# An attention and quantised-FFN layer on one core: loads spread, first queries stored first, roots moved to GpSimd, and two moves in the order of work

## The chip, the cores and the metric

The kernel runs on one core of a Trainium2 chip. The core has five engines with a queue of instructions each: TensorE (PE; its weight loads are shown as PEld), VectorE (DVE), ScalarE (ACT), GpSimd (POOL) and SyncE (SP, which here only issues transfers). Transfers are carried by 16 DMA engines; SP and POOL both issue them. An engine takes its instructions in order, and one that waits holds up all behind it. The metric is the device time of one execution in microseconds; the kernel before takes 1176.38 us (median of 3 runs, 1175.61 to 1177.49).

## The reference

`x` is (2, 1024, 512) in float32: two batches of 1024 tokens. Two layers follow each other, each on the layer norm of its input and added to it:

```python
q, k, v = proj(w_q), proj(w_k), proj(w_v)          # 32 heads of 16
attn = softmax(q @ k.T / sqrt(16))
x = x + (attn @ v) @ w_o.T

xq = int4_quant(layernorm(x))                      # rounded, clipped to -8..7
gate, up = bitlinear(xq, w_gate), bitlinear(xq, w_up)   # 512 -> 1376, weights -1, 0, 1
inter = int8_quant(up * square(relu(gate)))
x = x + bitlinear(inter, w_down)                   # 1376 -> 512
```

`int4_quant` divides by the mean absolute value of a row (beta), `int8_quant` by its largest absolute value (gamma). `bitlinear` divides a weight matrix by its mean absolute value (`w_mean`), rounds to -1, 0 or 1, and multiplies the product by `w_mean` and a scale. `w_mean` is needed of the three matrices before their first use.

## The kernel before

**Steps and slots.** The attention is cut into 32 steps: a batch, a half of its 512 queries (h), a group of 8 heads (g) and one half of that group (s), 4 heads at a time on PE. A step has 8 slots. In a slot T of the loop at the end of the kernel, PE computes scores for the maxima of one step (`max_mm`, L635, tiles `psm`), the scores for the exponentials of an older step, ten slots behind (`exp_mm`, L670, `pse`), and the products with the values of a still older one (L703, `pso`). DVE reduces `psm` to maxima (L645), ACT computes the exponentials `e` (L680). Scores stand in three pairs of PSUM banks, which are used in turn.

**Where the operands come from.** Projected queries and keys are split in a high and a low part (`hi`, `lo`) and stored to DRAM (`qD`, `kD`, L507 and L510), the values to `vD`; they come back in the layouts that the steps need: `kst` and `qst` for the maxima (L574, L580), `kw` (keys, two halves of four slots, L599) and `qm` (queries, L606) for the exponentials, `v` (L611), which POOL spreads into `vk` (L616). A step's row maxima become extra rows of `qm`: DVE combines them (`max_parts`, L650 to L653), PE transposes them (`max_rows`, L658, `psn`), ACT copies the row (L661) and POOL repeats it (L663).

**The start.** `norm_inputs` normalises the first batch's two halves (`fast`): means and variances on DVE, the inverse root by `inverse_root`, centring, PE transpositions. PE runs 40 warm-up matmuls (L1342) meanwhile. `project_qk` with `first` then projects the first keys and queries, and copies `hi` and `lo` straight into `kst` and `qst` of steps 0 and 1, in pieces of 16 rows (L500), by SP and POOL; after that it stores them to `qD` and `kD` (L507, L510). `upto` runs a generator until it yields a given word, and `now` to its end; their sequence sets the order of SP's and POOL's queues there.

**Fill.** All other work is a set of generators in `Fillers`. `fill.run(budget)` is called twice in a slot, once for short work and once with `share` (ns of PE time), and advances tasks that are ready, by their due slots. `("gap", n)` makes a task sleep for n such calls, so n / 2 slots. The background list holds the sums of the absolute weights (`weight_sums`, 35 blocks of up to 0.25 MB, loaded by POOL, L803, and summed by ACT, L817), then their quantising (`weight_quant`, POOL L859 and DVE L861, blocks loaded by POOL again). `norm_inputs` of the second batch is a task too: eight loads of 0.25 MB on SP (L365). `output_proj` (`psy`, L900, for two tiles of 128 tokens), `ffn_input`, `ffn_product` (gate `pg` and up `pu`, L989) and `ffn_output` (`py`, L1059) make the second layer for 12 of the 16 tiles of tokens. `fill.pace` gives the PE time per slot that meets all due slots; `share` is at least SHARE (960) and at most MORE (1800).

**The end.** The last four tiles are made in `the_end`, whose list (`Line`) is ordered by a planner: each generator names its next instruction's engine and modelled time, and the planner emits the one that can start first.

**The inverse root** (L336 to L353) is a bit trick and three Newton steps, 12 DVE operations on a few columns.

Of the kernel before, what the change touches and what calls it, by code (L numbers as in the profile page):

```python
# [10 lines left out]
F32 = mybir.dt.float32  # L11
# [222 lines left out]
def kernel(  # L234
# [66 lines left out]
    for i in range(4):  # L301
        nc.vector.memset(second[32 * i : 32 * i + 16, :], 0)
    negmagic = const.tile([P, 1], F32, name="negmagic")
# [33 lines left out]
    def inverse_root(dst, var, k, name):  # L337

        a = sp.tile([P, k], F32, tag="ra", name=f"ra_{name}")
        t = sp.tile([P, k], F32, tag="rt", name=f"rt_{name}")  # L340
        y = sp.tile([P, k], F32, tag="ry", name=f"ry_{name}")
        nc.vector.tensor_scalar(a, var, EPS, None, ALU.add)
        nc.vector.tensor_scalar(
            t.bitcast(I32), a.bitcast(I32), 1, None, ALU.logical_shift_right
        )
        nc.vector.tensor_scalar(
            y.bitcast(I32), t.bitcast(I32), -1, RSQRT_SEED, ALU.mult, ALU.add
        )
        for i in range(3):
            yield ("gap", 1, "light")  # L350
            nc.vector.tensor_tensor(t, y, y, ALU.mult)
            nc.vector.scalar_tensor_tensor(t, t, -0.5, a, ALU.mult, ALU.mult)
            nc.vector.scalar_tensor_tensor(dst if i == 2 else y, t, 1.5, y, ALU.add, ALU.mult)  # L353
# [3 lines left out]
    def norm_inputs(b, half, fast, need=()):  # L357
# [8 lines left out]
        yield ("gap", 4 if fast else 14)  # L366
# [10 lines left out]
        yield from inverse_root(r[:, c], mv[:, c, 1], n, f"1_{k}")  # L377
# [85 lines left out]
    def project_qk(b, g, which, h, have, fast=False, first=False):  # L463
# [25 lines left out]
        yield ("gap", 3)  # L489
        if first:  # L490

            for s in range(2 - which):
                for l, part in enumerate((hi, lo)):
                    for a in range(2 - which):
                        for r in range(4):
                            src = part[32 * r + 16 * s : 32 * r + 16 * s + 16, :].bitcast(F32)
                            at = 32 * r + 16 * (l if which else a)
                            dst = kst[0][:, h * QB : (h + 1) * QB] if which else qst[s][l]
                            queue = (nc.sync, nc.gpsimd)[l if which else a]
                            queue.dma_start(dst[at : at + 16, :].bitcast(F32), src)  # L500
                yield ("copied",)
        queue = nc.gpsimd if fast and not first else nc.sync
        for l, part in enumerate((hi, lo)):
# [7 lines left out]
            yield ("gap", 1)  # L511

# [293 lines left out]
    def weight_sums():  # L806
# [5 lines left out]
        for k in range(len(todo) + 4):  # L812
# [12 lines left out]
            yield ("gap", 2)  # L825
# [50 lines left out]
    def output_proj(b, h, tiles):  # L876
# [48 lines left out]
        nc.vector.tensor_scalar(neg, mv[:, :, 0], -1.0, None, ALU.mult)  # L925
        yield from inverse_root(r, mv[:, :, 1], w, f"2_{k}")
# [13 lines left out]
        nc.vector.tensor_scalar(cg, beta, wscale[0], None, ALU.mult)  # L940
        nc.vector.tensor_tensor(cg, cg, cg, ALU.mult)
        nc.vector.scalar_tensor_tensor(c3, beta, wscale[1], cg, ALU.mult, ALU.mult)
# [79 lines left out]

    def ffn_output(b, h, i, last):
# [72 lines left out]
    def the_end(n):  # L1096
# [208 lines left out]
        for k in range(2):  # L1305
            line.add(values(k))
            line.add(scales(k))
# [266 lines left out]
```

## Time and profile before

| | us |
|---|---|
| median of 3 runs | 1176.38 |
| profiled execution | 1175.35 |
| its span, first to last instruction | 1173.5 |
| PE busy | 1122.4 |
| DVE busy | 850.0 |
| ACT busy | 699.5 |
| POOL busy | 370.4 |

Engines overlap, so their busy times don't add up. A slice row of the page has 40 digits, each the busy tenths of 1/40 of the span. A line of waits reads: who waited, for whom, microseconds in total, times, the longest. A line of the chain of waits reads: start, length, and the instruction or transfer that set the time there. A line of the timeline reads: start, length, engine, line of the kernel, operation, tile written and tiles read, count, and in brackets the idle time before it and what ended it.

### The profile page before, as it was taken

What the parts mean: (1) busy time and instruction counts of PE and PEld (TensorE: products, weight loads), DVE (VectorE), ACT (ScalarE), POOL (GpSimd) and SP (SyncE); (2) the same over time, 40 slices, a digit from 0 to 9 for tenths busy, and PEclk for the clock granted to TensorE, in tenths of its full rate; (3) what the DMA queues carried; (4) which work ended last, traced back from release to release, by engine and by line L of the source; (5) the groups of instructions that cost most, each with busy time, mean ns of one, the idle gap of its engine ahead of it and who ended that gap; (6) DMA issues with size and microseconds to landing.
All of it is one profiled execution on the core that took longest, in us unless ns stands there. A gap on an engine that the chain in (4) does not pass through costs nothing.

```text
span 1173.5 us, 18117 instructions
## 1 busy us (share of the span) xinstructions
PE 1122.4 (96%) x6890; PEld 512.7 (44%) x6890; DVE 850.0 (72%) x1291; ACT 699.5 (60%) x894; POOL 370.4 (32%) x433
## 2 busy tenths in 40 slices
PE   8869999699999999999999999999999999999988
PEld 6524545245444545454454333333433434344344
DVE  5836566575877667776666889888888788996257
ACT  2026677476765656566555666666666565676646
POOL 4212234142446554751222123232113122242111
PEclk9889999799999999999999999999999999999999
DMA  5465568656554754655365453667775565543210
GB/s 154 132 154 150 181 182 242 142 147 195 165 141 147 191 157 155 168 167 128 102 174 142 104 116 88 124 132 122 129 114 119 117 127 120 118 96 72 75 27 37
DMA packets 107398, 157.12 MB, mean 134 GB/s; under 512 B 33720, under 2 KB 46488, under 8 KB 107312
## 3 DMA queue, kind: packets, MB, share of 16 engines
q1 hardware_dynamic: 95872, 129.39, 45.8%
q0 software_dynamic: 11440, 26.58, 8.4%
q8 instruction: 54, 0.88, 0.3%
q14 instruction: 32, 0.26, 0.1%
HBM read 114.41 MB, written 34.05 MB: 127 GB/s over the span
## 4 chain that ended last, share of the span: by engine, by line
PE 80%; DVE 10%; DMA 5%; ACT 3%; issue 1%; SPq 1%; POOL 0%; ACTq 0%; POOLq 0%; DVEq 0%
PE pse L670 21%; PE pso L703 18%; PE psm L635 13%; DVE pm L645 7%; PE psk L471 5%; PE psq L471 4%; PE psv L525 4%; PE psy L900 3%; PE py L1059 2%; DMA kw<-kD 2%; PE pu L989 2%; PE pg L989 2%; ACT e L680 1%; PE end L1215 1%; DMA kst<-kD 1%
## 5 line engine op out<-in xcount | busy, mean ns | idle before, releaser
L645 DVE TENSOR_REDUCE pm<-psm 128x2 f32<-128x1024 f32 x512 | 602.2, 1218 | 244.7 <-PE psm L635 243.8
L680 ACT ACTIVATE e<-pse 128x1024 f32<-128x1024 f32 x512 | 524.2, 1026 | 356.7 <-PE pse L670 350.2
L670 PE MATMUL pse<-qm,kw 72*128 72x512 f32 x1024 | 409.6, 483 | 24.5 <-DMA kw<-kD 19.2
L670 PEld LDWEIGHTS pse<-qm,kw 72*128 72x128 f32 x1024 | 169.0, 190 | 307.9 <-ACT e L680 196.9
L703 PE MATMUL pso<-e,vk 128*32 128x512 f32 x2048 | 274.4, 606 | 1.4 <-ACT e L680 1.4
L635 PE MATMUL psm<-kst,qst 32*128 32x512 f32 x2048 | 206.3, 449 | 9.6 <-DVE pm L645 5.1
L635 PEld LDWEIGHTS psm<-kst,qst 32*128 32x128 f32 x2048 | 88.0, 184 | 112.7 <-issue 62.4
L663 POOL CAST qm<-qm 8x1536 fp32r<-8x1536 f32 x32 | 46.9, 1467 | 115.1 <-ACT qm L661 56.4
L703 PEld LDWEIGHTS pso<-e,vk 128*32 128x32 f32 x2048 | 40.5, 108 | 96.2 <-issue 91.7
L1003 POOL TENSOR_TENSOR g<-g 128x460 f32<-128x460 f32 (+1 forms) x36 | 34.4, 955 | 136.7 <-ACT g L999 132.4
L714 ACT COPY po<-pso 64x512 f32<-64x512 f32 x64 | 37.1, 580 | 38.7 <-PE pso L703 38.7
L859 POOL TENSOR_SCALAR low<-raws,whalf 128x512 bf16<-128x512 f32 (+2 forms) x35 | 52.4, 1497 | 13.9 <-DVE pm L645 7.0
L525 PEld LDWEIGHTS psv<-wv,xnT 128*128 128x128 f32 x384 | 48.4, 192 | 2.9
L525 PE MATMUL psv<-wv,xnT 128*128 128x128 f32 x384 | 49.1, 275 | 0.0
L616 POOL COPY vk<-v 128x512 f32<-128x512 f32 x24 | 14.7, 611 | 105.4 <-DMA v<-vD 96.1
L471 PE MATMUL psk<-xnT,wk 128*128 128x512 f32 x96 | 47.7, 604 | 0.0
L471 PE MATMUL psq<-xnT,wq 128*128 128x512 f32 x96 | 47.2, 594 | 0.0
L900 PE MATMUL psy<-wo,po 128*128 128x512 f32 x96 | 46.6, 595 | 0.0
L989 PEld LDWEIGHTS <-xqT 128*128 128x128 bf16 x288 | 22.7, 99 | 30.7 <-issue 16.0
L1059 PE MATMUL py<-wd,iqT 128*128 128x512 fp8e4 (+1 forms) x132 | 32.2, 390 | 3.1 <-DMA iqT<-iq 3.1
L989 PE MATMUL pg<-wg,xqT 128*128 128x460 fp8e4 (+1 forms) x144 | 34.2, 360 | 0.0
L989 PE MATMUL pu<-wu,xqT 128*128 128x460 fp8e4 (+1 forms) x144 | 34.2, 360 | 0.0
(233 smaller groups left out, 975.9 us busy)
## 6 DMA issues: line engine op xcount, KB each, us to landing
kw<-kD SPq DMA_DIRECT2D x100, 256.0 KB
qm<-qD SPq DMA_DIRECT2D x32, 512.0 KB
qst<-qD SPq DMA_DIRECT2D x60, 256.0 KB
kst<-kD SPq DMA_DIRECT2D x24, 512.0 KB
qD<-hi_q SPq DMA_DIRECT2D x32, 256.0 KB
qD<-lo_q SPq DMA_DIRECT2D x32, 256.0 KB
v<-vD SPq DMA_DIRECT2D x24, 256.0 KB
x<-in_x SPq DMA_DIRECT2D x20, 256.0 KB
```

The source lines that it names most:

```text
L471: nc.tensor.matmul(ps, w[:, c, :], xnT[b, h][:, c, :], start=(c == 0), stop=(c == KC - 1))
L525: nc.tensor.matmul(ps[:, i * P : (i + 1) * P], xnT[b, half][:, c, i * P : (i + 1) * P], w[:, c, :], start=(c == 0), stop=(c == KC - 1),)
L635: nc.tensor.matmul(ps[:, r % 2, :], qst[n][l][rows, t * P : (t + 1) * P], kst[n][rows, kh * QB : (kh + 1) * QB], start=(l == 0), stop=(l = ...
L645: nc.vector.tensor_reduce(pm[n][:, t, kh, 2 * j : 2 * j + 2], ps, AX.X, ALU.max, negate=True)
L663: nc.gpsimd.tensor_copy(rows[:, 1:, :], rows[:, :1, :].bitcast(F32).to_broadcast([8, 3, QB]))
L670: nc.tensor.matmul(ps[:, r % 2, :], k[: MROW + 8, r, (i % TQ) * P : (i % TQ + 1) * P], qm[n][: MROW + 8, r, :], start=True, stop=True,)
L680: nc.scalar.activation(e, ps, AF.Exp, scale=SCALE)
L703: nc.tensor.matmul(acc[0][32 * r : 32 * r + 32, :], vk[steps[n][3]][:, 4 * i + r, :], e[:, r % 2, :], start=(i == 0), stop=(i == NT - 1),)
L859: nc.gpsimd.tensor_scalar(low, w, h[:rows, m, 1:2], None, ALU.is_lt)
L900: nc.tensor.matmul(ps, OT[b, h, g][:, i * P : (i + 1) * P], wo[g], start=(g == 0), stop=(g == NG - 1),)
L989: nc.tensor.matmul(ps, xT[:, c, :], w[:, c, n : n + size], start=(c == 0), stop=(c == KC - 1))
L1059: nc.tensor.matmul(py, iqT[:rows, c, :], wd[:rows, c, :], start=(c == 0), stop=(c == FC - 1))
```

## The change

Line numbers of the profile of before are those of the kernel before.

- `inverse_root` becomes two POOL operations, an addition and a power with the exponent -0.5 (a constant tile `minus_half`). It is used at the start (twice), in the second batch's norm (twice), in six output projections and twice in the end, where the planner's time for it goes from 2.5 us on DVE to 1.0 on POOL. Some other small operations go from DVE to POOL: `neg`, `cg` and `c3` in `output_proj`, the scaling of `gm` and `cd` in `ffn_output` (one DVE operation is merged there).
- `norm_inputs` of the second batch leaves a gap of 5 after each load of x, and a gap of 4 instead of 14 after them. `weight_sums` has a gap of 3 instead of 2.
- At the start the queries' stores to `qD` come before the second step's copies of them, and `qm` and the first half of `kw` are loaded there instead of in the loop.
- `max_rows` is issued after the fill of its slot instead of before it.
- `share` is at least 1500 from slot 138 on.
- The down product of tile 11, the last outside the end, is handed to the end's list (`late_down`).

```diff
-    def inverse_root(dst, var, k, name):
...
+    def inverse_root(dst, var):
+
+        nc.gpsimd.tensor_scalar(dst, var, EPS, None, ALU.add)
+        nc.gpsimd.tensor_tensor(dst, dst, minus_half[:, : dst.shape[1]], ALU.pow)
...
             nc.sync.dma_start(xs[i], x[b, t * P : (t + 1) * P, :])
-        yield ("gap", 4 if fast else 14)
+            if not fast:
+                yield ("gap", 5)
+        yield ("gap", 4)
...
+        def copies(s):
+            for l, part in enumerate((hi, lo)):
+                for a in range(2 - which):
+                    for r in range(4):
+                        src = part[32 * r + 16 * s : 32 * r + 16 * s + 16, :].bitcast(F32)
+                        at = 32 * r + 16 * (l if which else a)
+                        dst = kst[0][:, h * QB : (h + 1) * QB] if which else qst[s][l]
+                        by = (nc.sync, nc.gpsimd)[l if which else a]
+                        by.dma_start(dst[at : at + 16, :].bitcast(F32), src)
+
         if first:
-            for s in range(2 - which):
...
-                yield ("copied",)
+            copies(0)
+            yield ("copied",)
...
+        if first and not which:
+            yield ("stored",)
+            copies(1)
...
                 raw.append(load_raw(*todo[k], "raw"))
-            yield ("gap", 2)
+            yield ("gap", 3)
...
-        nc.vector.tensor_scalar(neg, mv[:, :, 0], -1.0, None, ALU.mult)
-        yield from inverse_root(r, mv[:, :, 1], w, f"2_{k}")
+        nc.gpsimd.tensor_scalar(neg, mv[:, :, 0], -1.0, None, ALU.mult)
+        inverse_root(r, mv[:, :, 1])
...
-        nc.vector.tensor_scalar(cg, beta, wscale[0], None, ALU.mult)
-        nc.vector.tensor_tensor(cg, cg, cg, ALU.mult)
-        nc.vector.scalar_tensor_tensor(c3, beta, wscale[1], cg, ALU.mult, ALU.mult)
+        nc.gpsimd.tensor_scalar(cg, beta, wscale[0], None, ALU.mult)
+        nc.gpsimd.tensor_tensor(cg, cg, cg, ALU.mult)
+        nc.gpsimd.tensor_scalar(c3, beta, wscale[1], None, ALU.mult)
+        nc.gpsimd.tensor_tensor(c3, c3, cg, ALU.mult)
...
-        nc.vector.tensor_scalar(gm, gm, c3, None, ALU.mult)
-        nc.vector.tensor_scalar(d, gm, EPS, None, ALU.add)
+        nc.vector.tensor_scalar(d, gm, c3, EPS, ALU.mult, ALU.add)
         nc.vector.reciprocal(d, d)
         yield ("gap", 1, "light")
+        nc.gpsimd.tensor_scalar(gm, gm, c3, 1.0 / 127.0, ALU.mult, ALU.mult)
+        nc.gpsimd.tensor_scalar(cd, gm, wscale[2], None, ALU.mult)
         nc.vector.tensor_scalar(f, d, 127.0, c3, ALU.mult, ALU.mult)
-        nc.vector.tensor_scalar(cd, gm, 1.0 / 127.0, wscale[2], ALU.mult, ALU.mult)
...
         nc.sync.dma_start_transpose(iqT, iq)
+        if order == (B * NQ - 1) * TQ - 1:
+            late.append((iqT, cd, x2.pop((b, h, i)), out[b, t * P : (t + 1) * P, :]))
+            return
...
-            yield "DVE", 2.5, {"done": f"rstd{k}"}
-            now(inverse_root(r[:, c], stats[:, c, 1], 2, f"2_end_{k}"))
+            yield "POOL", 1.0, {"done": f"rstd{k}"}
+            inverse_root(r[:, c], stats[:, c, 1])
...
+        def late_down():
+
+            ints, scale, xt, rows_out = late.pop()
+            yield "PE", 2.4, {"bank": True, "after": ("ints",)}
+            ps = line.bank
+            for c in range(FC):
+                rows = min(P, I - c * P)
+                nc.tensor.matmul(
+                    ps, ints[:rows, c, :], wd[:rows, c, :], start=(c == 0), stop=(c == FC - 1)
+                )
+            yield "DVE", 0.75, {"free": True}
+            y = sb.tile([P, H], F32, tag="tmp", name="y_late", bufs=3)
+            nc.vector.scalar_tensor_tensor(y, ps, scale, xt, ALU.mult, ALU.add)
+            nc.sync.dma_start(rows_out, y)
+
+        line.events["ints"] = 5.0
+        line.add(late_down())
...
     upto(queries, "copied")
     now(keys[0])
     now(firsts[1])
+    upto(keys[1], "copied")
+    upto(queries, "stored")
     now(keys[1])
+    load_qm(0)
+    now(queries)
     load_k(1)
-    now(queries)
+    load_kw(0, 0)
...
-        if im == 4 and nm < NSTEP:
+        if im == 4 and 0 < nm < NSTEP:
             load_qm(nm)
         n, p = divmod(T + 4 - LE, NT)
-        if 0 <= n < NSTEP and p % TQ == 0 and not same_keys(n):
+        if (n > 0 or p) and 0 <= n < NSTEP and p % TQ == 0 and not same_keys(n):
             load_kw(n, p // TQ)
...
-        if im == 0 and 0 < nm <= NSTEP:
-            max_rows(nm - 1)
-        share = min(max(fill.pace([w[4:] for w in ffns]), SHARE), MORE)
+        share = min(max(fill.pace([w[4:] for w in ffns]), SHARE if T < NT * NSTEP // 2 + LE else 1500.0), MORE)
         left = fill.run(share + min(left, SHARE))
+        if im == 0 and 0 < nm <= NSTEP:
+            max_rows(nm - 1)
```

More of the change, by code (lines that the diff above doesn't have):

```diff
@@ L302 @@
         nc.vector.memset(second[32 * i : 32 * i + 16, :], 0)
+    minus_half = const.tile([P, 4], F32, name="minus_half")
+    nc.gpsimd.memset(minus_half, -0.5)
     negmagic = const.tile([P, 1], F32, name="negmagic")
@@ L333, in spare @@
         return ps_o.tile([P, cols], dtype, tag="o", name=name)
-    def inverse_root(dst, var, k, name):
[L339 to L353, printed above, removed]
+    def inverse_root(dst, var):
+        nc.gpsimd.tensor_scalar(dst, var, EPS, None, ALU.add)
+        nc.gpsimd.tensor_tensor(dst, dst, minus_half[:, : dst.shape[1]], ALU.pow)
     xnT = {}
@@ L376, in norm_inputs @@
         c = slice(first, first + n)
-        yield from inverse_root(r[:, c], mv[:, c, 1], n, f"1_{k}")
+        inverse_root(r[:, c], mv[:, c, 1])
         yield ("gap", 0)
@@ L489, in project_qk @@
         yield ("gap", 3)
-        if first:
-            for s in range(2 - which):
[L493 to L500, printed above, removed]
-                yield ("copied",)
-        queue = nc.gpsimd if fast and not first else nc.sync
+        queue = nc.gpsimd if fast and not first else nc.sync
+        def copies(s):
[7 more added lines that the diff above has]
+                        by.dma_start(dst[at : at + 16, :].bitcast(F32), src)
+        if first:
+            copies(0)
+            yield ("copied",)
         for l, part in enumerate((hi, lo)):
@@ L1021, in ffn_product @@
         nc.vector.tensor_reduce(most[order], peaks.pop(order)[:, : len(chunks)], AX.X, ALU.max)
+    late = []
     def ffn_output(b, h, i, last):
@@ L1150, in scales @@
             nc.vector.tensor_scalar(neg[:, c], stats[:, c, 0], -1.0, None, ALU.mult)
-            yield "DVE", 2.5, {"done": f"rstd{k}"}
-            now(inverse_root(r[:, c], stats[:, c, 1], 2, f"2_end_{k}"))
-            yield "DVE", 0.8, {"after": (f"dev{2 * k}", f"dev{2 * k + 1}"), "done": f"scale{k}"}
+            yield "POOL", 1.0, {"done": f"rstd{k}"}
+            inverse_root(r[:, c], stats[:, c, 1])
+            yield "DVE", 0.8, {"after": (f"dev{2 * k}", f"dev{2 * k + 1}", f"rstd{k}"), "done": f"scale{k}"}
             nc.vector.scalar_tensor_tensor(beta[:, c], dev[:, c], 1.0 / H, r[:, c], ALU.mult, ALU.mult)
@@ L1516 @@
             weights_of(ne, ie, 0)
+        share = min(max(fill.pace([w[4:] for w in ffns]), SHARE if T < NT * NSTEP // 2 + LE else 1500.0), MORE)
+        left = fill.run(share + min(left, SHARE))
         if im == 0 and 0 < nm <= NSTEP:
             max_rows(nm - 1)
-        share = min(max(fill.pace([w[4:] for w in ffns]), SHARE), MORE)
-        left = fill.run(share + min(left, SHARE))
         if exps:
```

## The prediction

> **What bounds the kernel now.** I read the page's slices, then what the matrix engine (PE) waited for, then windows, chain and timeline around each hole, and the SP queue's own waits.
>
> ```profile
> span 1173.5 us, 18117 instructions
> PE   8869999699999999999999999999999999999988
> DMA  5465568656554754655365453667775565543210
> ```
>
> A slice is 29.3 us. PE is full except in the third (59 to 88 us), the eighth (205 to 235) and the edges. Its own waits and the windows name the holes (in a window: PE, PEld, DVE, ACT, POOL busy, granted clock, DMA share, GB/s):
>
> ```profile
> PE pse L670 <- DMA kw<-kD: 19.2, 2, 11.0
> PE psm L635 <- DMA qst<-hi_q: 3.5, 1, 3.5
> PE py L1059 <- DMA iqT<-iq: 3.1, 1, 3.1
> ```
>
> ```profile
> 34.00:74.00 40.00, 26.20 (x134) 13.97 (x126) 21.73 (x22) 3.36 (x5) 7.24 (x10) 0.80 0.54 131
> 214.00:237.00 23.00, 12.01 (x50) 4.93 (x49) 9.03 (x22) 5.91 (x9) 2.10 (x4) 0.70 0.53 118
> 237.00:610.00 373.00, 372.25 (x2405) 178.76 (x2403) 260.24 (x304) 233.52 (x286) 165.42 (x179) 1.00 0.58 157
> 686.00:735.00 49.00, 45.04 (x292) 17.53 (x284) 47.08 (x86) 31.48 (x41) 14.02 (x14) 1.00 0.40 93
> 1121.00:1174.00 53.00, 47.17 (x237) 23.48 (x236) 39.55 (x124) 31.90 (x67) 7.95 (x8) 0.98 0.07 26
> ```
>
> PE is idle 13.8 us in the first and 11.0 us in the second, and the clock falls there too (0.80, 0.70). From 237 to 610 us nothing is lost; from 686 to 735 DVE is the full engine (47.1 of 49). The chain of waits gives the transfers:
>
> ```profile
> 33.21 7.39 DMA kD<-lo_k
> 40.67 9.51 DMA kst<-kD
> 52.77 6.81 DMA qD<-lo_q
> ...
> 208.58 20.28 DMA kw<-kD
> ...
> 1114.24 3.53 DMA iqT<-iq
> 1117.82 3.59 PE py L1059 x11
> ```
>
> One more measure: a slot's length, the distance between the first exponentials (ACT e) of neighbouring slots in the timeline. A slot without fill takes 3.56 us (e at 892.29, 895.85, 899.41), with one gate or up product 3.59, one projection piece (two matmuls) 3.65, two pieces 4.51, a whole down product 5.19; a row transposition (psn) adds about 0.52. So an empty slot wastes almost a product, and only fill beyond one piece makes a slot longer.
>
> **The change, part by part.** The profiled execution took 1175.35 us (span 1173.5 and 1.85 around it), 1.0 under the median of the runs, 1176.38. The sum is made against 1175.35; the prediction adds the 1 us again.
>
> *First queries stored first.* Before, SP issues at 40.67 kst (step 1's keys), then 8 qst copies, 4 qD stores from 50.75, and only at 59.64 qm and then kw, since qm reads back qD. Its waits:
>
> ```profile
> SPq L574 <- DMA kD<-lo_k: 6.7, 1, 6.7
> SPq L606 <- DMA qD<-lo_q: 4.7, 1, 4.7
> SPq L500 <- DMA kst<-kD: 4.5, 1, 4.5
> ```
>
> The third says that SP holds no more than eight transfers in flight: the last qst copy, eight after kst, went out at 50.2, when kst had landed. After, the four qD stores follow the second keys' kst copies (done at 32.43) and take 1.34 + 2.04 us, so 35.8; the two kD stores go past them, 3.4 us later than now; qm waits for qD, which lands about 6 us behind (6.81 in the chain): 42. Behind that wait stand the 8 qst copies, then kst, kw and v. The eighth copy waits for qm (about 5.5 us: 47.5), kst goes out at 48.5 instead of 40.67, and at the same 7 to 9.5 us lands at 56 to 58. So step 1's first psm, now at 50.5, comes at about 56: a new wait of 5.5 us for kst in place of 3.5 for qst. But two slots later (4.9 and 3.6 us) pse finds kw and qm there: 56 + 8.5 + 1 = 65.5, e at 66.5 to 67.5, against pse at 67.94 and e at 71.64 now, the latter behind POOL's qm cast at 69.29. That cast now goes behind two POOL operations of psq (0.61 and 1.26), which fit in front of 65. Worth 4.5 us; ends: kst as slow as kw at 207 us (-1, a loss) and kst landing in 5 us (8 gained).
>
> *Bulk loads spread.* kw went out at 207.2 and landed at 228.9; slot 45 took 16.04 us instead of 4.51 and slot 46 5.99 instead of 3.65 at half clock, 13.9 us together. In front of it SP had 8 loads of x (0.25 MB each, 168 to 175 us); POOL one weight block per slot beside it (the DMA view of 140 to 240 us shows 18.4 MB). SP's issues swell from 0.4 us to 7.1 and 5.9 before kw: its queue is full. After, by the order of the instructions, five of the eight x loads stand before this kw and the blocks come every 1.5 slots: by then some 11 instead of 17. Less in front of kw: 3 x 0.25 + 6 x 0.25 = 2.2 MB, at the 150 to 200 GB/s of that stretch 11 to 15 us, and kw was 11 us late. The three x loads behind kw meet wq, qm and wv, which are due four slots later. I take 11.5 us; ends 0 (the queue is full anyway) and 13.9. The sums end at slot 82 instead of 63 and the quantising after 52 slots more, at about 135; the first gate product is at slot 157. If that cover were gone, products would start late by as many slots.
>
> *Roots and small products to POOL.* Per output projection 12 DVE operations of the root (about 2.5 us), three of c3 (0.267 + 0.16 + 0.289) and neg go, six times; per tile gm and cd (0.2 each), twelve times: 6 x 3.4 + 12 x 0.4 = 25 us of DVE. POOL gets some 75 operations; its nearest row is the 128x4 sum of "pick", 0.194 us; the power itself has no row. Bounds: that 0.194 and the 1.47 us of its 8x1536 cast; I take 0.5, nearer the row of the same shape. DVE's gain counts only where DVE sets the slot. Over slots 140 to 254 the slots are 9 us longer than the median of their kind; of this I give 2 to the roots; ends 9 and -5. At the start the root ends at 9.97, but PE's warm-up runs until 10.88 and the centring needs 0.5: nothing is won, and up to 2.2 us of power nothing lost. In POOL's queue a root may stand behind a wait for a division's DMA (longest 6.6 us); the DVE operation that reads it comes two slots (7.2 us) later.
>
> The timeline shows what such a move can cost. While POOL works on two inputs, a 128x2 DVE operation of 0.16 us takes 0.86 and ends with it:
>
> ```profile
> 705.89 0.95 POOL L1003 TENSOR_TENSOR g<-g 128x460 f32<-128x460 f32 x1 [5.95 <-ACT g L999]
> 705.99 0.86 DVE L351 TENSOR_TENSOR rt<-ry 128x2 f32<-128x2 f32 x1
> 706.88 0.16 DVE L352 SCALAR_TENSOR_TENSOR rt<-rt,ra 128x2 f32<-128x2 f32 x1
> ```
>
> By rows, 75 operations of 0.2 us are 15 us of such blocking if every one met DVE; I use a third for the -5. The Trainium skill speaks against this part in "GPSIMD Engine Reference", Key points: POOL shares its SBUF interfaces with VectorE, and contends with instructions that have two SBUF inputs. The rows above agree with it. The same page (Instruction dispatch) says that the first call of a freshly loaded kernel pays about 6 us; no POOL row here shows that ("pick" took 0.194), and by it the start alone would lose some 4 us.
>
> *Rows behind other work.* psn is issued after the fill. PE's weight load waited 6.2 us in all for DVE in front of it, PE 2.7. Slots with psn are 4.4 us over their kind's median in all. But its copy on ACT (0.58) now stands behind the fill's copy (0.59) and just before the bank is needed again: up to 0.25 us in 32 slots. Net 1 us gained; ends 7 and -8.
>
> *More fill from slot 138 and the down product in the end's list.* The order says where fill now stands. Slots 140 to 255, priced by the kinds above, get 7.6 us longer: one more empty slot, five more with a product, ten fewer with one output piece, five more with two, two more whole downs and three split ones fewer (3.56 + 5 x 3.59 - 10 x 3.66 + 5 x 4.50 + 2 x 5.19 - 3.56 - 2 x 4.55 = 5.1), and the psn slots, fuller by 2.5. Slots 256 to 262 fall from 24.2 to 22.3 (only one down left, the rest 2.9 each): -1.9. From the last slot's e (1109.0) to the end's first transposition (1121.2) now lie py8, py3, the wait for iqT (1114.24 to 1117.8) and 11 matmuls at half clock (3.59). After, pse, pso, the last psy, pso and the copy remain, 4 us: -8.2. Together -2.5. In the end's list the 11 matmuls cost 2.4 us (their row at full clock), since PE is busy there from 1121 to 1145; two roots (2.3 each) leave DVE, full from 1140 to 1165, but the deviations on ACT end only 0.5 us before the first root: +1, ends +4 and -2.
>
> **Sum.** 1175.35 - 4.5 - 11.5 - 2 - 1 - 2.5 + 1 = 1154.9; with the 1 us to the median, rounded, 1155.5.
>
> **The rivals.**
> A: the queue stays full, kw is as late as now. For it: wq, qm, qD and kw alone are 2 MB in that stretch. Against it: the DMA share falls to 0.4 to 0.6 between 195 and 202 us, so the stretch before is drained by fewer loads. Time: 1155.5 + 11.5 = 1167.
> B: kst takes the place of kw at the start, so that nothing is won there. For it: kst goes behind a wait and eight copies; against it: qm and kw have 8.5 us more. Time: 1155.5 + 4.5 = 1160.
> C, the slower side: a slow power. It is on the path at the start (free up to 2.2 us) and twice in the end (free to about 2.5, by the slack to the next PE work), and from 6 us on in six projections, where DVE waits with the maxima behind it. At 7 us: 4.8 + 9 + 6 = 20, which cancels everything; at 8 us 5.8 + 11 + 12 = 29, 1184. Against it: POOL's 128x4 sum in 0.194 us.
>
> **How the numbers follow.** Forecast 0.66, A 0.12, B 0.13, C 0.07, unnamed 0.02. The range takes in A and B and a good part of the ends: 1155.5 - 10.5 (a whole kw stall and 8 us at the start) = 1145, and A with 5 us of POOL's blocking = 1172. The likeliest alone is 1149 to 1162. Faster by over 0.2% (2.3 us, about what a measurement here can tell from no change) are forecast, A and B, less a little for their ends: 0.89; same 0.03, slower 0.08.
>
> **What would show it.** Step 1's first psm at 54 to 58 us, waiting for kst, and the first e at 65 to 69. No PE wait over 3 us for kw near 207 us, clock 1.00 there. POOL rows of the power under 1 us. No "py <- iqT" wait before the end's list, its length 52 to 55 us. Wrong would make it: a power of several us, a new long kw or qm wait in slots 45 to 56, or maxima waiting for a DVE that waits for POOL.

## The result and the profile after

The changed kernel takes 1190.2 us (median, 1188.2 to 1193.9) against 1176.8 of the kernel before, timed beside it: ratio 1.0119, 95% interval 1.0092 to 1.0145. It is 1.2% slower, where the prediction had 1155.5 us and the range 1145 to 1172. The page's head of the changed kernel:

```profile
span 1188.2 us, 17993 instructions
PE   8669999999999999999999999999999999998996
...
PEclk9879999999999999999999998999999999999798
```

A slice is 29.7 us. The hole in the eighth slice is gone. The clock row (`PEclk`) has three dips that before did not have: 8 in the 25th digit, 7 in the 38th and 8 in the last. In the third slice it is deeper (7 for 8). Lines of after are numbered differently from before (`psm` L635 is now L631, `pse` L670 is L666, the row's copy `qm` L661 is L657). What PE waited for in after (microseconds in total, times, the longest):

```profile
PE psm L631 <- DMA kst<-kD: 18.7, 1, 18.7
PE pse L666 <- ACT e L676: 5.9, 20, 0.4
PE end L1280 <- ACT end_kw L1275: 4.3, 1, 4.3
PE psm L631 <- ACT qm L657: 3.3, 9, 0.8
...
PE pg L986 <- DVE inter L1009: 2.5, 1, 2.5
```

The 19.2 us for `kw` have left the list. A wait of 18.7 us for `kst` takes their first half's place. Two kinds of wait are new, for the row's copy on ACT and for `inter`, and that for ACT in the end's list (`end_kw`) has grown from 0.2 to 4.3 us. Laid beside before, by the first exponential of a slot in both timelines, and by the steps of the prediction (all in us):

| stretch | before | after | difference | predicted |
|---|---|---|---|---|
| start to slot 11 | 76.8 | 81.3 | +4.5 | -4.5 |
| slots 11 to 44 | 137.5 | 139.1 | +1.6 | -1 for all the rows |
| slots 45 and 46 | 22.0 | 8.2 | -13.9 | -11.5 |
| slots 47 to 139 | 375.6 | 381.4 | +5.8 | 0 |
| slots 140 to 255 | 464.3 | 474.8 | +10.5 | +7.6 - 2 |
| slots 256 to 263 | 29.0 | 33.8 | +4.9 | -1.9 |
| slot 264 to the end's list | 16.0 | 8.5 | -7.5 | -8.2 |
| the end's list | 52.3 | 61.0 | +8.7 | +1 |
| sum | 1173.5 | 1188.2 | +14.6 | -20.5 |

Only the two lines that take something away came out near the prediction. Everything else was paid for, in six places.

The start. The chain of waits of after (start, length, what set the time):

```profile
37.28 10.17 DMA qD<-lo_q
...
47.53 6.99 DMA qm<-qD
...
55.09 13.21 DMA kst<-kD
68.43 1.71 PE psm L631 x8
```

`kst` goes out at 55.1, takes 13.2 us and lets step 1's first `psm` begin at 68.4. Before, it began at 50.5.

The eighth slice. The same window of before, then of after (PE, PEld, DVE, ACT, POOL busy, granted clock, DMA share, GB/s):

```profile
205.00:245.00 40.00, 29.01 (x163) 12.95 (x156) 23.53 (x45) 18.34 (x32) 9.59 (x14) 0.83 0.60 145
```

```profile
205.00:245.00 40.00, 39.39 (x252) 18.57 (x252) 27.01 (x32) 27.76 (x42) 12.22 (x18) 1.00 0.67 187
```

PE is busy for 39.4 of 40 us and the clock stays at 1.00. Here the change did what it was predicted to do.

Slot 169, 8.99 us long where the next one takes 3.59 (in before it took 4.45). The timeline of after (start, length, engine, line, operation, and in brackets the idle time before it and what ended it):

```profile
727.76 0.61 POOL L612 COPY vk<-v 128x512 f32<-128x512 f32 x1 [11.05 <-DMA v<-vD]
728.34 0.94 POOL L1000 TENSOR_TENSOR g<-g 128x456 f32<-128x456 f32 x1
...
729.31 0.63 DVE L1009 TENSOR_TENSOR inter<-pu,g 128x456 f32<-128x456 f32 x1 [5.26 <-POOL g L1000]
...
730.00 1.69 PE L986 MATMUL pg<-wg,xqT 128*128 128x460 fp8e4 x4 [2.52 <-DVE inter L1009]
```

POOL stands 11 us in front of its copy of `v`, whose load took 10.58 us; the `g` behind it is late, DVE's `inter` waits 5.3 us for `g`, and PE for `inter`. The clock then falls to a half for 6.8 us. In before the same copy waited 3.1 us, as the load was there 4.6 us after its issue at 714.80:

```profile
719.42 0.61 POOL L616 COPY vk<-v 128x512 f32<-128x512 f32 x1 [3.10 <-DMA v<-vD]
```

The prediction has no such term.

The slots near 1100 us, in stretches of 3.4 us, columns as above:

```profile
1091.00:1094.40 3.40, 3.40 (x20) 1.32 (x18) 0.75 (x1) 1.62 (x2) 0.63 (x1) 1.00 0.12 26
1094.40:1097.80 3.40, 1.86 (x12) 0.74 (x12) 0.00 (x0) 3.33 (x6) 1.28 (x1) 1.00 0.40 139
1097.80:1101.20 3.40, 3.40 (x16) 2.09 (x16) 0.68 (x2) 1.96 (x3) 0.00 (x0) 0.51 0.68 122
1101.20:1104.60 3.40, 3.40 (x12) 1.19 (x8) 0.00 (x0) 1.35 (x2) 0.00 (x0) 0.50 0.85 295
1104.60:1108.00 3.40, 3.08 (x11) 0.96 (x11) 0.00 (x0) 1.55 (x2) 0.00 (x0) 0.50 0.01 2
1108.00:1111.50 3.50, 3.18 (x12) 0.70 (x11) 0.00 (x0) 1.94 (x2) 0.00 (x0) 0.50 0.00 0
...
1114.90:1118.30 3.40, 3.40 (x16) 1.39 (x15) 0.69 (x1) 1.02 (x1) 0.00 (x0) 1.00 0.00 0
```

In the second stretch PE works 1.86 of 3.4 us while ACT is full (3.33): two halves of `iq` stand in front of `e`. The clock then falls to a half for 17.1 us, and slots without fill take 4.26 us instead of 2.9. (Slots this late have no maxima to compute, so they are shorter than the 3.56 us of the others.)

### The profile page after: what moved, and what is told of

It is laid out like the page before. It is cut to its first block, busy times and chain, and to the rows that moved or that the text cites. A ratio compares the mean times of both kernels' runs of the same rounds, so it can differ in the third digit from the quotient of the medians.

```text
span 1188.2 us, 17993 instructions
## 1 busy us (share of the span) xinstructions
PE 1131.8 (95%) x6890; PEld 516.6 (43%) x6890; DVE 823.6 (69%) x1100; ACT 697.9 (59%) x893; POOL 396.9 (33%) x512
## 4 chain that ended last, share of the span: by engine, by line
PE 79%; ACT 8%; DVE 5%; DMA 5%; issue 2%; POOL 1%; SPq 1%; ACTq 0%; POOLq 0%
PE pse L666 21%; PE pso L699 18%; PE psm L631 13%; PE psk L462 4%; PE psq L462 4%; ACT e L676 4%; PE psv L521 4%; PE psy L896 3%; DVE pm L641 3%; PE py L1061 2%; PE pu L986 2%; PE pg L986 2%; DMA kst<-kD 1%; DMA v<-vD 1%; DMA qD<-lo_q 1%
## 5 line engine op out<-in xcount | busy, mean ns | idle before, releaser
L666 PE MATMUL pse<-qm,kw 72*128 72x512 f32 x1024 | 405.4, 479 | 8.5 <-ACT e L676 5.9
L666 PEld LDWEIGHTS pse<-qm,kw 72*128 72x128 f32 x1024 | 169.5, 191 | 281.8 <-ACT e L676 206.6
L699 PE MATMUL pso<-e,vk 128*32 128x512 f32 x2048 | 277.4, 612 | 4.0 <-ACT e L676 3.3
L631 PE MATMUL psm<-kst,qst 32*128 32x512 f32 x2048 | 209.4, 449 | 25.1 <-DMA kst<-kD 18.7
L631 PEld LDWEIGHTS psm<-kst,qst 32*128 32x128 f32 x2048 | 88.0, 184 | 128.8 <-issue 84.3
L1009 DVE TENSOR_TENSOR inter<-pu,g 128x460 f32<-128x460 f32 (+1 forms) x36 | 22.7, 630 | 12.4 <-PE pu L986 7.1
```

Of the source, the lines that this page charges most:

```text
L631: nc.tensor.matmul(ps[:, r % 2, :], qst[n][l][rows, t * P : (t + 1) * P], kst[n][rows, kh * QB : (kh + 1) * QB], start=(l == 0), stop=(l = ...
L666: nc.tensor.matmul(ps[:, r % 2, :], k[: MROW + 8, r, (i % TQ) * P : (i % TQ + 1) * P], qm[n][: MROW + 8, r, :], start=True, stop=True,)
L699: nc.tensor.matmul(acc[0][32 * r : 32 * r + 32, :], vk[steps[n][3]][:, 4 * i + r, :], e[:, r % 2, :], start=(i == 0), stop=(i == NT - 1),)
```

## The experiments

The six parts of the change are separate edits; put together they give the changed kernel exactly. Most kernels below are the kernel before with one of them, and the diff is that part of the change. Ratios are against the kernel before, timed beside each.

**The start's order alone** (`copies(1)` behind the stores to `qD`, `load_qm(0)` and `load_kw(0, 0)` at the start):

```diff
+    upto(keys[1], "copied")
+    upto(queries, "stored")
     now(keys[1])
-    load_k(1)
+    load_qm(0)
     now(queries)
+    load_k(1)
+    load_kw(0, 0)
```

> Only the start's new order, all else as before. Theory (the start itself loses): step 1's first psm waits for kst until about 68 us instead of for qst until 50.5, the first e comes at 77 instead of 71.6, and slot 11 starts 4.5 us late; the stall for kw near 207 us stays, since it comes from the loads in front of kw, so the time is 1176.8 + 4.5 = 1181. Rival (my prediction's step: kst lands at 56 to 58, first e at 67): 1172; that the late kst in the whole change came from the spread loads or the roots beside it would also give about 1172.

1179.6 us, ratio 1.0028 (1.0010 to 1.0047). Its chain:

```profile
37.27 9.87 DMA qD<-lo_q
...
47.22 6.52 DMA qm<-qD
...
54.31 13.95 DMA kst<-kD
```

The same three transfers in the same time as in the whole change, so the late `kst` is the order's own doing, not that of the parts beside it. The size needs care. Slot 11 begins at 76.8 in before's profile, and at 78.0 to 82.2 in the six other profiles here with the same instructions up to there. Two with the row's copy moved have 81.5 and 82.1, and five with the roots on POOL 74.6 to 81.1. With the new start it is 79.8 to 81.5 in five profiles. The middles of the old order's fourteen and the new one's five, 78.4 and 80.8, are 2.4 us apart, and the ratio gives 3.3. So of the 4.5 us between the two profiles a part is chance: before's profile shows an early start.

**Keys first in the new start**, on a kernel described further down (spread loads and the loop's roots on POOL):

```diff
+    load_k(1)
     load_qm(0)
     now(queries)
-    load_k(1)
```

> On the spread loads with the loop's roots on POOL: the start of the change, but with step 1's keys (kst) loaded ahead of qm and the second copies of the queries. Theory (kst is late because it stands behind qm's wait and eight copies): psm of step 1 at 58 to 60 us, first e at 67 to 69, so 3 to 5 us under the same kernel with the start of before: 1158 to 1160. Rival (whatever stands last in SP's queue is late, now qst or kw): first e at 72 or later, 1162 or more.

1163.6 us, ratio 0.9898 (0.9870 to 0.9925); the same kernel with the start of before has 0.9877 (0.9851 to 0.9903). No gain. Its chain:

```profile
49.65 11.33 DMA kst<-kD
...
60.99 2.36 DMA qst<-lo_q
...
63.43 2.42 PE psm L649 x8
```

`kst` lands 7 us earlier, and now the seventh of the eight `qst` copies, which goes out only when `kst` has landed, holds the same `psm`. The first `e` comes at 72.9, which is 4 us before the changed kernel's 77.1, but not before the 69.5 to 74.6 of the kernels with the old order and the roots on POOL. The rival is right: all of these transfers are needed for steps 0 and 1, and those that stand last in SP's queue are late.

**The rows alone** (`max_rows` behind the fill):

```diff
-        if im == 0 and 0 < nm <= NSTEP:
-            max_rows(nm - 1)
...
         left = fill.run(share + min(left, SHARE))
+        if im == 0 and 0 < nm <= NSTEP:
+            max_rows(nm - 1)
```

> Only max_rows moved behind the fill. Theory (the row's copy on ACT behind the fill's copy holds the pair of banks that the next psm needs): psn slots of the projection phase go from 4.17 to about 4.6 and some to 5.2 us, a wait of psm for ACT's qm copy appears, some 8 us over 256 slots: 1184 to 1185. Rival (the longer psn slots of the whole change came from the weight sums' copies that the spread loads move into them): 1176 to 1177, or 1175 by my prediction's step.

1184.6 us, ratio 1.0064 (1.0043 to 1.0086). Six of the fourteen psn slots from 32 to 136 take 4.64 us instead of 4.17, and the slots from 140 to 255 take 2.7 us more.

**Only the copy moved**: the transposition stays in front of the fill, its copy goes behind.

```diff
         if im == 0 and 0 < nm <= NSTEP:
-            max_rows(nm - 1)
+            max_rows(nm - 1)      # the transposition only
...
         left = fill.run(share + min(left, SHARE))
+        if im == 0 and 0 < nm <= NSTEP:
+            copy_rows(nm - 1)     # nc.scalar.copy and POOL's repetition
```

> On the kernel before: the transposition psn stays in front of the fill, and only its copy on ACT and POOL's repetition are issued behind the fill. Theory (the copy's place behind the fill's copy is what costs, since it frees the pair of banks): psn slots as in the moved rows alone, 4.6 us and more where they were 4.17, a wait of psm for ACT's qm copy of some 3 us, and 4 to 5 us more between slots 70 and 256: 1181 to 1185. Rival (PE's own place of the transposition costs): 1176 to 1178.

1186.3 us, ratio 1.0076 (1.0038 to 1.0115). What PE waited for there:

```profile
PE psm L635 <- ACT qm L667: 4.6, 10, 0.9
```

So it is the copy's place, not the transposition's. The timeline of slot 32 shows it, ACT's in before, then ACT's and PE's in the changed kernel:

```profile
160.92 1.02 ACT L680 ACTIVATE e<-pse 128x1024 f32<-128x1024 f32 x1 [0.75 <-PE pse L670]
161.97 0.58 ACT L661 CAST qm<-psn 8x512 fp32r<-8x512 f32 x1
162.57 0.59 ACT L484 COPY full_k<-psk 128x512 f32<-128x512 f32 x1
```

```profile
165.53 1.02 ACT L676 ACTIVATE e<-pse 128x1024 f32<-128x1024 f32 x1 [1.35 <-PE pse L666]
166.46 0.62 ACT L813 ACTIVATE junk<-raw 128x512 bf16<-128x512 f32 x1
...
167.07 0.57 ACT L475 COPY full_k<-psk 128x512 f32<-128x512 f32 x1
167.67 0.58 ACT L657 CAST qm<-psn 8x512 fp32r<-8x512 f32 x1
...
168.30 0.73 PE L631 MATMUL psm<-kst,qst 32*128 32x512 f32 x6 [0.80 <-ACT qm L657]
```

In before the row's copy comes right behind `e`. In the changed kernel a weight sum, the fill's copy and only then the row's copy follow `e`, and `psm` starts the moment that this ends.

**The spread loads alone, then each half of them:**

```diff
             nc.sync.dma_start(xs[i], x[b, t * P : (t + 1) * P, :])
-        yield ("gap", 4 if fast else 14)
+            if not fast:
+                yield ("gap", 5)         # only_xgap and only_loads
+        yield ("gap", 4)
...
                 raw.append(load_raw(*todo[k], "raw"))
-            yield ("gap", 2)
+            yield ("gap", 3)             # only_wgap and only_loads
```

> Only the spread bulk loads. Theory (as in the whole change): slots 45 and 46 are 4.5 and 3.7 us, no wait for kw near 207 us, 13.9 us gained, less 1 to 2 us for the sums' copies in more slots: 1176.8 - 12.5 = 1164. Rival (the stall goes only because the new start loads qm and kw early): the stall stays and the time is 1174 to 1177.

> On the kernel before: only the second batch's loads of x are spread (gap 5 after each, 4 in place of 14 behind them); the weight sums as before. Theory 1 (x, in kw's own queue on SP, is what delays it): slots 45 and 46 take 8 to 9 us instead of 22, time 1164 to 1168. Theory 2 (the weight blocks on POOL's queue take the DMA engines' share): 0.75 of 2.2 MB less, so a third of the stall goes, 1171 to 1174.

> On the kernel before: only the weight sums' blocks come every three calls of the fill instead of two; x as before. Theory 1 (x is what delays kw): the stall stays at 10 us or more, 1175 to 1178. Theory 2 (the weight blocks are): two thirds of the stall go, slots 45 and 46 take 11 to 13 us, 1167 to 1171.

| kernel | us | ratio | slots 45 + 46 | slots 47 to 139 |
|---|---|---|---|---|
| before | 1176.8 | | 22.0 | 375.6 |
| both | 1171.3 | 0.9943 (0.9920 to 0.9965) | 8.2 | 379.8 |
| x only | 1171.9 | 0.9937 (0.9912 to 0.9962) | 15.5 | 376.2 |
| weight blocks only | 1180.4 | 1.0010 (0.9980 to 1.0040) | 18.9 | 381.2 |

The stall goes by 13.9 us with both and by 6.5 with `x` alone, so theory 2's arithmetic for `x` (a third) was low. That the blocks alone take 3.2 away is not shown: in eight kernels with the loads of before, slots 45 and 46 take anything from 17.7 to 22.8 us. The blocks' profile is also the slowest of its ten runs (1190.7 us), with 5.4 us more in slots 141 to 143 that no other kernel has. Two thirds, as theory 2 had it for the blocks, is far too high. In the ten profiles with both, the stall is gone in nine and 3.3 us long in one (`after_keep`).

The loads were expected to bring 12.5 us and brought 6.7, and both together are no faster than `x` alone: with the blocks spread, slots 47 to 139 take 4.2 us more. The sums' two ACT operations (0.62 us in the rows above, and 0.19 to read the sum) now last until slot 78 instead of 59. In slot 56 they stand beside a row's copy and a fill's copy, and it takes 4.79 us instead of 4.17; slots 65 and 66 take 4.2 instead of 3.56. But 2.9 of the 4.2 us lie in slots 82, 120 and 124, behind the last sum: in 82 the mean is made from the sums (in 63 before), and the quantising runs until slot 136 instead of 116. The other kernels with spread blocks and the old place of the rows have 2.8 to 7.4 us more in this stretch, slot 124 alone between 4.5 and 7.8 us.

**The roots and small products on POOL, everywhere** (as in the change, `neg`, `c3`, `gm` and `cd` with them):

```diff
-            nc.vector.tensor_tensor(t, y, y, ALU.mult)      # and the other 11
+        nc.gpsimd.tensor_scalar(dst, var, EPS, None, ALU.add)
+        nc.gpsimd.tensor_tensor(dst, dst, minus_half[:, : dst.shape[1]], ALU.pow)
...
-            yield "DVE", 2.5, {"done": f"rstd{k}"}
+            yield "POOL", 1.0, {"done": f"rstd{k}"}
```

> Only the roots and small products on POOL. Theory 1 (the end's list is longer because the root is on POOL, which changes the planner's order): end's list 58 to 61 us instead of 52.3, time 1182 to 1186. Theory 2 (the list is longer because of the late down product, the roots cost nothing there): list 51 to 53 us and the time 1174 to 1177. In both POOL's power takes 0.7 us for 128x2 and 1.0 for 128x4.

1174.1 us, ratio 0.9975 (0.9953 to 0.9998). Two opposite sums: slots 140 to 255 take 6.1 us less than before, and the end's list takes 59.9 us instead of 52.3. The list is theory 1's, the time theory 2's. The power takes 0.73 us (128x2) and 1.04 us (128x4), in the changed kernel:

```profile
L342 POOL TENSOR_TENSOR rstd<-rstd,minus_half 128x2 f32<-128x2 f32 x6 | 4.4, 728 | 0.5
L342 POOL TENSOR_TENSOR rstd<-rstd,minus_half 128x4 f32<-128x4 f32 x4 | 4.2, 1044 | 0.3
```

**The spread loads with the roots on POOL in the loop, the end's list as before**, and then **the end's roots on POOL too, but told to the planner as before** (`old_root` is the bit trick; the first kernel has it in the end, the second the last line):

```diff
             yield "DVE", 2.5, {"done": f"rstd{k}"}
-            now(old_root(r[:, c], stats[:, c, 1], 2, f"2_end_{k}"))
+            inverse_root(r[:, c], stats[:, c, 1])
```

> Spread bulk loads together with the roots and small products on POOL, but the end's list with its roots on DVE as before; start, rows, share and last down product as before. Theory (both gains are real and lie in different slots, 6 to 7 us at slots 45 to 47 and 5 to 6 us in slots 150 to 255): list 52 us, 1176.8 - 12 = 1165. Rival (they are gains of one kind, fill that comes at a better time, and don't add): 1168 to 1171.

1162.3 us, ratio 0.9877 (0.9851 to 0.9903). The list takes 52.1 us. Against the loads alone that is 0.0066 or 7.8 us for the loop's roots (the intervals allow about 4 to 12), and slots 140 to 255 take 6.2 us less. So the two gains add.

> On the spread loads with the loop's roots on POOL: the end's two roots also on POOL, but told to the planner as 2.5 us of DVE, so that the end's list keeps the order of before. Theory (the list got longer because the planner's order changed): list 50 to 52.5 us, time 1160 to 1163. Rival (the power on POOL itself is too slow for the list): list 58 us or more, 1168 to 1170.

1162.5 us, ratio 0.9893 (0.9851 to 0.9935), the list 52.3 us. With POOL's power in it but the order of before, the list is as short as before. The 7.6 us are the planner's new order, not the operation's price. In the chain of the roots-alone kernel one sees what the order does: the last tile's last gate and up come behind other tiles' down products, and its whole tail then runs by itself:

```profile
1162.54 0.63 DVE end_xnT L1227
...
1163.83 0.55 DVE highs L1229
...
1166.00 0.73 ACT end_kw L1263
...
1168.37 4.71 PE end_o L1287 x11
```

PE is busy for 0.19 of the 3.4 us from 1162.7 on, the granted clock is 0.50 behind it, and the last 11 matmuls take 4.71 us; in the list of before they take 2.56 at a clock of 1.00.

**The late down product alone, then with the good parts, then later in the list:**

```diff
+        if order == (B * NQ - 1) * TQ - 1:
+            late.append((iqT, cd, x2.pop((b, h, i)), out[b, t * P : (t + 1) * P, :]))
+            return
...
+        line.events["ints"] = 5.0        # 35.0 in late_35
+        line.add(late_down())
```

> Only the last down product in the end's list, the roots there on DVE. Theory (the list's length comes from the roots, as they alone gave 59.9 us against 52.3): the list takes 53 to 55 us, the way to it is 8 us shorter, 1170 to 1172. Rival (the late product puts the planner's order off as well): list 58 us or more, 1175 to 1180.

1173.8 us, ratio 0.9974 (0.9950 to 0.9997). The list is 56.3 us long, 4.0 more, and the way to it 5.8 shorter. That lies between the theory's list (53 to 55) and the rival's (58 or more).

> On the spread loads with the loop's roots on POOL: the last down product in the end's list. Theory (its gain of 2 to 4 us adds, path to the list 6 us shorter and the list 4 longer): 1159 to 1161. Rival (the list's order depends on what else is in it, and the gain goes): 1162 to 1165.

1159.4 us, ratio 0.9855 (0.9829 to 0.9882), list 56.5 us. This is the fastest kernel here, 17 us under before and 31 under the changed kernel. That the late product is what put it 3 us under the same without it is not shown: the two intervals overlap.

> Spread loads, loop's roots on POOL and the late down product, which the planner may take only 35 us into the list instead of 5. Theory (PE is full in the list's first 25 us, so the product costs its 2.4 us and an order besides): list 52.5 to 55 us instead of 56.5, 1156 to 1158.5. Rival (any other content upsets the greedy order): list 56 us or more, 1159 or more.

1162.6 us, ratio 0.9874 (0.9829 to 0.9919), list 59.9 us. The rival is right. A product that can start 35 us into the list doesn't fill a hole but turns the order over, as the roots did. Lists of 52.0 to 52.4 us have the order of before; the others have 56.3 to 61.2.

**The share alone, then with the late down product:**

```diff
-        share = min(max(fill.pace([w[4:] for w in ffns]), SHARE), MORE)
+        share = min(max(fill.pace([w[4:] for w in ffns]), SHARE if T < NT * NSTEP // 2 + LE else 1500.0), MORE)
```

> Only the share of at least 1500 from slot 138 on. By the prediction's prices slots 140 to 255 get some 7.6 us longer and slots 256 to 262 some 2 shorter: 1182 to 1183. Theory (the emptied slots at the end lose the clock, and denser fill brings its own stalls): slots 256 to 263 don't get shorter but 3 to 5 us longer, granted clock under 0.9 there, 1186 to 1190. Rival (the roots on POOL and the moved rows, not the share, make slots 140 to 255 longer in the whole change): 1175 to 1178.

1181.2 us, ratio 1.0029 (1.0012 to 1.0047). Slots 140 to 255 take 474.7 us instead of 464.3, slots 256 to 263 26.9 instead of 29.0, and the way from there to the list is 5.8 us shorter, as the last down product's integers are ready earlier.

> Share and late down product together on the kernel before. Theory (only both together empty slots 256 to 262 so far that PE idles for ACT and the clock falls): slots 256 to 263 take 32 to 34 us instead of 29, granted clock under 0.9 there; slots 140 to 255 some 10 us longer, path to the list 8 us shorter, list 4 us longer: 1176.8 + 10 + 4 - 8 + 4 = 1187. Rival (the clock falls through something else in the whole change): slots 256 to 263 at 27 us, clock 1.00, 1180 to 1182.

1183.9 us, ratio 1.0056 (1.0032 to 1.0079). The theory falls, though the time lies between the two: slots 256 to 263 take 26.9 us, and the clock there is 1.00:

```profile
1090.00:1112.00 22.00, 18.91 (x102) 7.81 (x95) 4.16 (x14) 16.11 (x18) 4.29 (x5) 1.00 0.39 114
```

Here the emptied slots, with PE busy for 18.9 of 22 us, don't lose the clock. What the two gain at the end is largely one gain: each shortens the way to the list by 6 us alone, both together by 7.5 (from slot 264: 8.5 us instead of 16.0), while the list's 4 us remain.

**Matmuls that keep PE busy in slots 256 to 262 of the changed kernel:**

```diff
+        if 256 <= T <= 262:
+            ps = spare(f"keep_{T}")
+            for k in range(6):
+                nc.tensor.matmul(ps[:, :P], identr, identr, start=True, stop=True)
         if exps:
             weights_of(ne, ie, 1)
```

> The changed kernel with six more matmuls of 128 columns in each of the slots 256 to 262, whose result nobody reads. Theory (PE idles there for ACT, and the granted clock falls to a half for it): the clock stays at 1.00 and slots 259 to 263 take 17 to 19 us instead of 22.6, so 1190.2 - 4.5 = 1186, though PE has more to do. Rival (the clock falls for another reason, or the slots are bound by ACT and not by the clock): no gain, 1190 to 1193.

1187.9 us, ratio 1.0092 (1.0067 to 1.0117). The clock stays at 1.00 and slots 259 to 263 take 17.8 us instead of 22.7; slot 258 takes 7.1 instead of 5.4. That agrees with PE's idleness as the cause. The whole time's gain of 2 us can't be told from none, as the intervals overlap.

**`v`'s copy on POOL issued two slots later, in the changed kernel:**

```diff
         load_v(n)
-        yield ("gap", 2)
+        yield ("gap", 6)
         spread_v(n)
```

> The changed kernel with the spreading of v on POOL issued two slots later after its load. Theory (POOL stands at v's copy for 11 us and g, inter and pg behind it): slot 169 goes from 9.0 to 4.5 us or less, 1190.2 - 4.5 = 1185.5. Rival (v's copy is needed there anyway, or the stall moves to another slot): 1189 to 1192.

1179.2 us, ratio 1.0023 (0.9988 to 1.0057): 11 us less than the changed kernel, over twice what was expected. Slot 169 takes 3.59 us. The load of `v` is no faster (issued at 718.1), but POOL comes to the copy later and waits there for 0.57 us:

```profile
728.25 0.61 POOL L612 COPY vk<-v 128x512 f32<-128x512 f32 x1 [0.57 <-DMA v<-vD]
```

The other half comes from the slots near 1100 us, which have the same fill and the same 1.54 us wait for `e`, but lose the clock for 3.4 us and not for 17. That this is the edit's doing is not shown; it may be chance, with one profile of each kernel:

```profile
1090.60:1094.00 3.40, 1.86 (x12) 0.55 (x11) 0.00 (x0) 3.35 (x5) 1.27 (x1) 0.99 0.28 89
1094.00:1097.40 3.40, 3.40 (x16) 1.61 (x14) 0.68 (x2) 2.31 (x3) 0.00 (x0) 0.50 0.77 148
1097.40:1100.80 3.40, 2.69 (x17) 0.94 (x14) 0.00 (x0) 1.96 (x3) 0.00 (x0) 1.00 0.78 267
```

**Three parts taken out of the changed kernel** (rows, share and the end's roots put back):

```diff
-            yield "POOL", 1.0, {"done": f"rstd{k}"}
-            inverse_root(r[:, c], stats[:, c, 1])
+            yield "DVE", 2.5, {"done": f"rstd{k}"}
+            now(old_root(r[:, c], stats[:, c, 1], 2, f"2_end_{k}"))
...
+        if im == 0 and 0 < nm <= NSTEP:
+            max_rows(nm - 1)
-        share = min(max(fill.pace([w[4:] for w in ffns]), SHARE if T < NT * NSTEP // 2 + LE else 1500.0), MORE)
+        share = min(max(fill.pace([w[4:] for w in ffns]), SHARE), MORE)
         left = fill.run(share + min(left, SHARE))
-        if im == 0 and 0 < nm <= NSTEP:
-            max_rows(nm - 1)
```

> The changed kernel with three parts put back: rows in front of the fill, share as before, the end's roots on DVE. Kept: start, loads, the loop's roots, late down product. Theory (these three, with the clock, make the whole loss): 1159.4 for the same without the start, and 1 to 3 us for the start: 1160 to 1163. Rival (parts that gain alone lose together): 1167 or more.

1164.1 us, ratio 0.9889 (0.9842 to 0.9935). 26 us of the changed kernel's time go with three edits. It stands 4.7 us over the same without the new start, which is above the 1160 to 1163 that were expected and under the rival's 1167.

## Why the prediction was wrong

**First queries stored first: -4.5 predicted, +3.3 by its own run.** The step that failed is the arrival of `kst` (out at 48.5, landed at 56 to 58). The wait itself was foreseen, as was that `kw` and `qm` would no longer be waited for. But `qD` landed at 47.5 and not 42, since its 10.2 us were priced at 6 by a row of 6.8. The last copy waited 7.0 us for `qm` instead of 5.5, so `kst` went out at 55.1, and its 13.2 us were priced at 7 to 9.5. Three durations, two of them some 4 to 6 us low and one 1.5. The first `e` came at 77.1 and not 66.5 to 67.5. Rival B had named the mechanism and stopped at "nothing is won". The eight transfers that the prediction gave SP come from the program: in the traces SP's transfers set eight semaphores in turn (100 to 107), and one waits for the semaphore that it sets again. In before the last copy at 50.20 waits for semaphore 105, which `kst` had taken.

**Bulk loads spread: -11.5 predicted, -13.9 in the two slots, -6.7 in all.** The stall's mechanism and size were right, and the clock stayed at 1.00 as said. What failed is the cover of the longer sums. The step asked only whether products would start late (they did not) and gave the sums' operations on ACT, and the quantising behind them, no cost. Spread blocks cost 4.2 us in slots 47 to 139, and with them the loads are no faster than with `x` alone. Rival A is out: `kw` is in time.

**Roots on POOL: -2 predicted; -6 in the loop, and the list's part below.** The power is a little dearer than taken (0.73 and 1.04 against 0.5), and rival C's 7 us are far. Of the 9 us that slots 140 to 254 were over the median of their kind, 2 were given to the roots, and 6.1 went (464.3 to 458.3 us in slots 140 to 255). The direction was right and the size was low. The Trainium skill ("GPSIMD Engine Reference", Key points) had been weighed against this part: POOL shares its interfaces to SBUF with DVE and contends with DVE instructions that have two inputs there. After agrees: a DVE operation with two inputs that else takes 0.16 us takes 0.84 beside POOL's `g` (`a` on L933, longest 839 ns). But the sum says that relieving DVE is worth more. The same page (Instruction dispatch) has some 6 us for the first call of a freshly loaded kernel. No run here shows that: the power's first execution began 0.1 us behind the addition, at 7.48 us, and took 1.05 us, the second of the same shape 1.03.

**Rows behind other work: -1 predicted, +7.5 by its own run.** The step had the right object: "its copy on ACT (0.58) now stands behind the fill's copy (0.59) and just before the bank is needed again". It priced the wait at "up to 0.25 us in 32 slots". Where it shows, it is mostly 0.47 (4.64 for 4.17). In slots 32 and 56 of the changed kernel it is 1.07, of which 0.62 come with the spread loads alone (4.79), as a weight sum stands there too. `rows_split` shows that the copy alone does it. The predicted gain came from DVE waits of 2.7 us in all, so it could never have been large; the cost should have been taken from the fuller ACT slots.

**More fill from slot 138, and the late product: -2.5 and +1 predicted, +6.6 by their own run.** The prices by kinds of slot were fair outside the end's list: 10.4 us more in slots 140 to 255 for 7.6, 2.1 less in 256 to 263 for 1.9, 7.5 less before the list for 8.2. The failing step is the end's list, "+1, ends +4 and -2". 2.4 us of matmuls were priced, and the relief of DVE by two roots; the list was thought to keep its order. The planner is greedy: each of the two edits gives another order, which costs 4.0 and 7.6 us, and both together 8.7.

**What had no term at all.** POOL's 11 us in front of `vk`, with `g`, `inter` and `pg` behind it, and the half clock near 1100 us. They were 5.4 and some 5 of the 14.6 us between the two profiles; with `v`'s copy later the first was gone and the second short, and that kernel is not distinguishable from before. The prediction had named the queue ("in POOL's queue a root may stand behind a wait for a division's DMA") but looked at what the roots wait for, not at what new neighbours the moved fill gives the waits already there. Before, the same copy had waited 3.1 us, and POOL was still ready 1.3 us before the next `g` was.

The sum: by their own runs the start gives +3.3, the loads -6.7, the roots -2.9, the rows +7.5, share and late product together +6.6 us, in all about 8 of the 13.4 that were lost. The rest appears only together. `after_vgap` gets back 11.0, more than that rest, so the single effects add up to the whole only within some 5 us; each carries an interval of 2 to 4 us.

Two of the prediction's figures don't follow from its own terms. 1154.9 and 1.0 make 1155.9, not 1155.5. And a kw stall gone whole (2.4 more) with 8 us at the start (3.5 more) lie 5.9 us under the forecast, not 10.5. Neither bears on the miss.

## What to carry to other kernels

An operation that is moved behind others on an in-order engine costs what then stands in front of it in its fullest slot, and that must be read for the resource that it frees (here a pair of PSUM banks), not for the engine that it leaves. Where a greedy planner or a budget writes the order, any edit of its list is a new order: compile it and read it, or tell the planner the old costs, before pricing the operation itself. And a gain that is measured in one place (13.9 us here) has to be followed to the end, since the work that was spread has to be done somewhere.

## What the runs showed of the hardware

The half clock comes in steps. Its stretches after the start are 6.8, 10.2, 13.7 and 3.4 us long in before and 20.5, 6.8, 17.1 and 6.8 in after, all multiples of 3.41 us. The Trainium skill ("TensorE: Matmul & The Clock Gate", Part 1) has a free-running window of 3413 ns, and this agrees. The same section says that a window of idleness brings the half clock and a busy window brings the full one back. Here a stretch with PE busy for 1.86 of 3.4 us was enough to lose it, while 2.69 of 3.4 was not (the last row of the kernel with `v`'s copy later). That is no threshold: the changed kernel kept the full clock behind a stretch with 1.89 of 3.4 us (1152.5 to 1155.9). Nor did one busy stretch always bring it back. In after four more stretches followed the first at half clock although PE shows 3.40, 3.40, 3.08, 3.18 us busy in the first four. Before shows 3.40 us busy at half clock from 50.8 on, and another stretch at half clock behind it. In `after_vgap` one full stretch was enough. Why they differ stays open.

A transfer's time at the start does not follow from its size: `kst`, 0.5 MB, took 9.5 us in before, 11.3 with the keys first, 13.2 and 14.0 behind the copies. And a start with the same instructions ended, by slot 11, anywhere from 76.8 to 82.2 us (seven profiles), so that one profile of it carries a doubt of some 5 us.
